# A cross-attention kernel: per-batch choice of block products, and where a bank is written back and a sum is formed

## The chip, the cores and the metric

The kernel runs on one core of a Trainium2 chip. The time is the device time of one execution in microseconds, median of three runs; lower is better. The core has TensorE for matrix products (PE in the profile; PEld is its weight load), VectorE (DVE), ScalarE (ACT), GpSimd (POOL) and SyncE (SP, here only a queue that issues DMAs). Each works off its own instructions in program order and waits for the others by semaphores.

## The reference

Eight batches of cross attention with a residual. Everything is float32. `x1` and `x2` are 512 x 1024 for each batch.

```python
def _L0_xattn_ref(x1, x2, Wq, bq, Wk, bk, Wv, bv):
    q = jnp.einsum('bcn,dc->bnd', x1, Wq) + bq
    k = jnp.einsum('bcn,dc->bdn', x2, Wk) + bk[:, None]
    v = jnp.einsum('bcn,dc->bdn', x2, Wv) + bv[:, None]
    attn = jax.nn.softmax(jnp.einsum('bnd,bdm->bnm', q, k), axis=2)
    attn_out = jnp.einsum('bcm,bnm->bcn', v, attn)
    return attn_out + x1
```

B = 8, C = 512, N = 1024, D = 64.

## The kernel before

The scores stand transposed (m on the partitions, n along the row), in two halves of n (`h` 0 and 1), each with four steps `i` of 2 x 128 rows. The kernel does not form v. It first multiplies x2 with the unnormalized exponentials (stage "y", inner dimension 1024), scales by the reciprocal of the column sums, and then multiplies Wv with that (stage "o", inner dimension 512). Both are 512 x 1024 results and both are done by a Strassen-Winograd scheme of seven products of quarters instead of eight (`MULT`, L382): product 1 is 11 by 11, product 2 is 12 by 21, 6 is S2 by T2, 7 is S3 by T3, 5 is S1 by T1, 3 is S4 by 22, 4 is 22 by T4. The S are sums of x2's quarters (`a` in the code), the T are sums of the quarters of the exponentials (`t`). S1 = 21 + 22, S2 = 11 - S1, S4 = 12 + S2, S3 = 11 - 21; T1 = 12 - 11, T2 = T1 - 22 with the signs of the code, T3 = 22 - 12, T4 = 21 + T2.

A product of the stage "y" can be done in two ways. **Whole**: `multiply` (L392), two rows j of 128, four inner steps each, 128x512 matmuls, onto the bank pair it belongs to; for products 1, 6, 5 ScalarE copies the bank's partial result into a tile `u6` or `u5` (L418). **In blocks**: the same seven-product scheme once more inside the product, with 128x256 matmuls: seven `inner_product`s (L470). It needs four sums of the left quarter (`inner_left`, L439, four VectorE instructions of 128x256) and the sums of the right one (`inner_right`, L451, one of 128x1024 and two of 128x512). There are two kinds of block products. `multiply_seeded` (L491) opens the banks: ScalarE copies partial results into them (L511), and `complete` adds a last part on VectorE (L517). `multiply_onto` (L521) adds onto banks that hold something, and collects the rest in a tile `d` (ScalarE copies, L483) with a `complete` on VectorE (L551). `multiply_joined` (L560) is that, plus two `join`s (L566) on VectorE that add the bank to `d`: afterwards `d` holds the running sum, and the bank does not. `reseed` (L570) has ScalarE write `d` back into the two `a` banks, so that the next product can go on from there.

`period` (L811) does one batch. `n`, `nn`, `nnn` are the next three. Work of the next batch stands inside: its scores (`scores_and`), maxima (`folds`, `fold_halves`, `highest`), exponentials. Batch numbers in the text count from the first (`s.b` = 0) to the eighth or last (`s.b` = 7). The line `six` (L814) says in which batches product 6 is done in blocks: the third to the sixth, and the last. Product 5 is done in blocks in all but the first. In the seventh there is no `nn`, in the last there is no `n`.

From the second batch on the order is: product 1 and 2 in blocks (`multiply_seeded`), with the folds for the sum of the second half's exponentials on VectorE (`adds`) and `total` (an all-reduce over partitions on GpSimd, L288, with a small DMA behind it); then 6, the scores of the next batch's first half, 5, 7, 3, the second half's scores, 4, and the stage "o". `hooks` are functions that are called between the inner products, which puts their instructions there in ScalarE's and GpSimd's order.

T3 is formed in place of the quarter 12: ScalarE negates half of it (`sum_t3`, L352), and a DMA from GpSimd's queue adds the quarter 22 (L356). The folds for the sum read the quarter 12 too. T4: ScalarE copies the quarter 21 (`copy_t4`, L346) and a DMA adds T2 (L350). S4: SyncE loads the quarter 12 (`begin_s4`, L167), a DMA on GpSimd's queue adds S2 (`end_s4`, L171). These DMAs move 512 KB each. All DMAs that add are on GpSimd's queue; so are those of the denominators: `invert` writes a row to DRAM (L298), `spread` reads it back to all partitions (L303). In the last batch T3 is formed by VectorE instead (`sum_e(s, "T3")`, two instructions at L331).

The banks: PSUM holds two double buffers `sc` (scores, and the two working buffers of a block product) and the pairs `a` and `c`. The second half's scores use the pair `a` for step 2 (L966); it has to be empty then, which `evict_t3` (L580, L583) does after product 3. `copy_u1` (L358) keeps product 1's banks in a tile, `evict_y` forms the quarters of the result, `scale_y` multiplies by the reciprocals.

`weave` (L274) emits lists of steps by turns. The order on each engine is the order in the program; no planner changes it.

Of the kernel before, what the change touches and what calls it, by code (L numbers as in the profile page):

```python
# [12 lines left out]
ALU = mybir.AluOpType  # L13
# [3 lines left out]
def kernel(  # L17
# [151 lines left out]
    def end_s4(s):  # L169

        nc.gpsimd.dma_start(s.a["S4"], s.a["S2"], accum_op=ALU.add)  # L171
# [98 lines left out]
    def folds(s, h, kind, op):  # L270

        return [lambda i=i: fold(s, h, i, kind, op) for i in range(1, MH)]

    def weave(*rows):  # L274

        for steps in zip_longest(*rows):
            for step in steps:
                if step:
                    step()
# [78 lines left out]
    def copy_u1(s, j):  # L358
        if j == 0:
            s.tmp[1] = sb.tile([P, 2, H], F32, tag="y21", name=f"uy1_{s.b}")  # L360
        nc.scalar.copy(s.tmp[1][:, j, :], s.bank["a", j])
# [77 lines left out]
    def inner_left(s, i, x, tag):  # L439

        v = {f"{p + 1}{q + 1}": x[:, ts(q, MH // 2), ts(p, P)] for p in range(2) for q in range(2)}
        sums = sb.tile([P, 4, MH // 2, P], F32, tag=tag, name=f"aI{i}_{s.b}")
        v |= {step[0]: sums[:, z] for z, step in enumerate(LEFT)}
        s.inner[i] = v

        def make(k, x, y, op):
            return lambda: nc.vector.tensor_tensor(v[k], v[x], v[y], op)

        return [make(*step) for step in LEFT]
# [110 lines left out]
    def multiply_joined(s, i, v_tag, hooks={}):  # L560

        s.tmp[i], complete = multiply_onto(s, i, f"u{i}", v_tag, hooks)

        def join(j):
            d = s.tmp[i][:, j, :]
            nc.vector.tensor_tensor(d, s.bank["a", j], d, ALU.add)  # L566

        return [complete, lambda: join(0), lambda: join(1)]

    def reseed(s):  # L570

        for j in range(2):
            nc.scalar.copy(s.bank["a", j], s.tmp[6][:, j, :])

    def copy_7(s, j):
        if j == 0:
# [234 lines left out]
    def period(s, n, nn, nnn):  # L811

        late = s.b >= 1
        six = late and (n is None or s.b >= 2 and nn is not None)  # L814

        def first(i):
            multiply(s, "y", i, s.a, s.t, MH)
# [19 lines left out]
        def scores_0():  # L837
            then = scores_and(n, 0, 1, "c", next_queries if nn else nothing)
            if six:
                reseed(s)  # L840
            return then

        def add_exponential(i):
# [44 lines left out]
            scale_y(s, "T3", "11", "22")  # L888
        else:
            complete_1 = multiply_seeded(s, 1, "y11")  # L890
            adds = folds(s, 1, "sum", ALU.add)
            if six:
                weave(
                    adds,
                    [nothing, complete_1] + inner_right(s, 6, s.t["T2"], "yT1", "yT2"),
                    [nothing, nothing] + inner_left(s, 6, s.a["S2"], "i2"),
                )
            else:
                weave(adds, [nothing, complete_1] + inner_left(s, 7, s.a["S3"], "yT4"))
            total(s, 1)  # L900
            hooks = {5: lambda: copy_u1(s, 0), 4: lambda: copy_u1(s, 1)}
            if n:
                hooks |= {6: lambda: sum_t3(s, 0), 3: lambda: sum_t3(s, 2)}
            complete_2 = multiply_seeded(s, 2, "y22", hooks)
            complete_2()
            evict_y(s, "11")
            invert(s, 0)
            begin_s4(s)
            end_s4(s)
            sum_t4(s)  # L910
            evict_q = None
            if six:
                hooks = {6: lambda: copy_t4(s, 0), 5: lambda: copy_t4(s, 2)}
                complete_6, *join_6 = multiply_joined(s, 6, "v", hooks)
                lefts_5 = [] if n else inner_left(s, 5, s.a["S1"], "a11")
                weave(
                    inner_right(s, 5, s.t["T1"], "y21", "u1"), lefts_5, inner_left(s, 7, s.a["S3"], "yT4")
                )
                complete_6()
                weave(join_6)  # L920
                if n:
                    evict_q = scores_0()
                    weave(inner_left(s, 5, s.a["S1"], "i2"))
                    weave(folds(n, 0, "max", ALU.max))
                else:
                    reseed(s)
                    sum_e(s, "T3")
            else:
                copy_t4(s, 0)
                copy_t4(s, 2)  # L930
                first(6)
                weave(inner_right(s, 5, s.t["T1"], "y21", "u1"), inner_left(s, 5, s.a["S1"], "i2"))
                evict_q = scores_0()
                weave(folds(n, 0, "max", ALU.max))
            rights_7 = inner_right(s, 7, s.t["T3"], "yT1", "yT2")
            weave(rights_7, [nothing, nothing] + inner_left(s, 3, s.a["S4"], "aI3"))
            complete_5, *join_5 = multiply_joined(s, 5, "r", {6: evict_q} if nn else {})
            complete_5()
            if n:
                fold_halves(n, 0, ALU.max)  # L940
                highest(n, 0)
            spread(s, 0)
            shares(s, 1)
            weave(join_5, inner_right(s, 3, s.t["22"], "eT1"))
            if n:
                lower(n, 0, 0)
            complete_7 = multiply_seeded(s, 7, "y12")
# [167 lines left out]
```

## Time and profile before

| what | value |
|---|---|
| median of 3 runs | 685.12 us (684.97 to 685.27) |
| profiled execution, its time | 684.92 us |
| its span, first to last instruction | 683.1 us |
| granted TensorE clock, mean | 0.997 |
| ScalarE busy | 345.8 us, 51% |
| GpSimd busy | 217.7 us, 32% |
| GpSimd's DMA queue (q0) | 58.27 MB, 47.3% of 16 engines' span |
| SyncE's DMA queue (q1) | 79.31 MB, 32.0% |
| DMA L356 (T3), 12 of 512 KB, issue to landing | 6.0 us median |
| DMA L171 (S4), 7 of 512 KB | 8.6 us median |
| DMA L350 (T4), 14 of 512 KB | 12.1 us median |

How to read it: a busy share is that of the whole span; the page's timeline gives for each instruction its start, its duration, and in brackets the idle time of its engine just before it with what ended that. Durations overlap their successors a little, so the steps from start to start are what counts: four 128x256 matmul instructions show 1.03 us and follow each other every 0.863.

### The profile page before, as it was taken

How to read it: one execution, taken by the hardware profiler on the slowest of the kernel's cores; microseconds unless marked ns; L12 is line 12 of the kernel's file. 1: busy time of each engine (PE TensorE's matmuls, PEld its weight loads, DVE VectorE, ACT ScalarE, POOL GpSimd, SP SyncE). 2: the span in 40 equal slices, each digit the busy share in tenths (PEclk: the TensorE clock that was granted, in tenths of full speed). 3: DMA queues.
4: the chain of work that ended last, by engine and by line, in shares of the span. 5: the costliest groups of instructions: out<-in, count | busy, mean ns of one | idle time of the engine just before them, and what ended most of it. 6: DMA issues, size and time to landing. Idle time of an engine off the chain costs nothing.

```text
span 683.1 us, 7499 instructions
## 1 busy us (share of the span) xinstructions
PE 669.0 (98%) x2504; PEld 415.0 (61%) x2504; DVE 625.4 (92%) x826; ACT 345.8 (51%) x595; POOL 217.7 (32%) x189
## 2 busy tenths in 40 slices
PE   9999999999999999999999999999999999995997
PEld 5333554756558665668647685486755676474863
DVE  1999998989999999999999999999999889999884
ACT  2734266546455564473754656545645548443320
POOL 0124215341435314451144512434143621443100
PEclk9999999999999999999999999999999999999999
DMA  9666658997996969969699796998789784498503
GB/s 302 267 204 228 153 214 146 253 192 229 249 246 186 228 181 292 227 183 262 172 277 237 162 284 171 257 249 155 233 197 192 222 174 73 93 207 264 120 14 110
DMA packets 52790, 138.45 MB, mean 203 GB/s; under 512 B 5776, under 2 KB 8080, under 8 KB 52752
## 3 DMA queue, kind: packets, MB, share of 16 engines
q0 software_dynamic: 23472, 58.27, 47.3%
q1 hardware_dynamic: 28992, 79.31, 32.0%
q10 hardware_dynamic: 288, 0.39, 0.2%
q8 instruction: 20, 0.33, 0.2%
q14 instruction: 18, 0.15, 0.1%
HBM read 90.97 MB, written 16.81 MB: 158 GB/s over the span
## 4 chain that ended last, share of the span: by engine, by line
PE 93%; DVE 4%; DMA 1%; ACT 1%; issue 1%; SPq 0%; DVEq 0%; ACTq 0%
PE ps_oa L407 12%; PE ps_ya L474 10%; PE ps_oc L407 8%; PE ps_yc L474 8%; PE ps_s L240 6%; PE ps_ya L407 5%; PE ps_o L407 4%; PE ps_o L427 4%; PE ps_q L193 4%; PE ps_k L193 3%; PE ps_i4chain L474 3%; PE ps_i3chain L474 3%; PE ps_i5chain L474 3%; PE ps_i7chain L474 3%; PE ps_i1chain L474 3%; PE ps_i2chain L474 2%
## 5 line engine op out<-in xcount | busy, mean ns | idle before, releaser
L288 POOL PARTITION_ALL_REDUCE den<-half x16 | 51.6, 3225 | 91.2 <-DVE half L268 91.2
L283 POOL PARTITION_ALL_REDUCE top<-max x16 | 31.7, 1980 | 131.3 <-DVE few L296 58.2
L318 DVE TENSOR_TENSOR e<-e,top 128x1024 f32<-128x1024 f32 x60 | 69.8, 1213 | 0.0
L322 ACT ACTIVATE e<-e 128x1024 f32<-128x1024 f32 x60 | 61.8, 1057 | 6.2 <-DVE e L318 5.5
L407 PE MATMUL ps_oa<-yT,w_S 128*128 128x512 f32 x128 | 57.5, 592 | 0.0
L407 PE MATMUL ps_oc<-yT,w 128*128 128x512 f32 x128 | 57.4, 592 | 0.0
L667 POOL DMA_DIRECT2D sum<-e x21 | 28.9, 1377 | 84.3 <-ACT sum L672 36.1
L249 ACT COPY e<-ps_s 128x1024 f32<-128x1024 f32 x46 | 45.6, 1031 | 12.2 <-PE ps_s L240 7.2
L240 PE MATMUL ps_s<-q,k 64*128 64x512 f32 x188 | 47.8, 608 | 0.9 <-ACT q L693 0.8
L407 PEld LDWEIGHTS ps_oa<-yT,w_S 128*128 128x128 f32 x128 | 24.3, 190 | 30.6 <-issue 30.6
L407 PEld LDWEIGHTS ps_oc<-yT,w 128*128 128x128 f32 x128 | 24.3, 190 | 30.6 <-issue 29.9
L260 DVE TENSOR_TENSOR max<-max,e 128x1024 f32<-128x1024 f32 x30 | 36.7, 1222 | 2.2 <-DVE max L260 0.5
L418 ACT COPY uo<-ps_oa 128x512 f32<-128x512 f32 x32 | 18.7, 585 | 35.1 <-PE ps_oa L407 34.0
L240 PEld LDWEIGHTS ps_s<-q,k 64*128 64x128 f32 x188 | 17.0, 186 | 23.0 <-issue 16.3
L511 ACT COPY ps_ya<-ps_i1chain 128x256 f32<-128x256 f32 x28 | 10.0, 357 | 40.8 <-PE ps_i1chain L474 37.3
L588 DVE TENSOR_TENSOR y<-y,den 128x1024 f32<-128x1024 f32 x24 | 30.4, 1293 | 0.3
L407 PE MATMUL ps_oa<-y,w_S 128*128 128x512 f32 (+1 forms) x68 | 28.8, 567 | 0.0
L407 PE MATMUL ps_o<-y,w 128*128 128x512 f32 x64 | 28.8, 592 | 0.0
L427 PE MATMUL ps_o<-y,w 128*128 128x512 f32 x64 | 28.8, 592 | 0.0
L407 PE MATMUL ps_ya<-eT,aS 128*128 128x512 f32 x64 | 28.3, 595 | 0.0
L193 PE MATMUL ps_k<-x_in_x_dram,wqk_sb 128*64 128x512 f32 x112 | 26.0, 600 | 0.4 <-DMA x_in_x_dram<-in_x_dram 0.4
L331 DVE TENSOR_TENSOR eT<-eT,e 128x1024 f32<-128x1024 f32 x16 | 26.1, 1637 | 0.0
(217 smaller groups left out, 1655.1 us busy)
## 6 DMA issues: line engine op xcount, KB each, us to landing
x_in_x_dram<-in_x_dram SPq DMA_DIRECT2D x60, 512.0 KB, 8.4
a<-in_x2T_dram SPq DMA_DIRECT2D x32, 512.0 KB, 9.9
sum<-e POOLq DMA_DIRECT2D x21, 512.0 KB, 9.1
aS<-in_x2T_dram SPq DMA_DIRECT2D x14, 512.0 KB, 6.3
aS<-in_x2T_dram POOLq DMA_DIRECT2D x14, 512.0 KB, 7.6
uo<-in_x_dram POOLq DMA_DIRECT2D x14, 512.0 KB, 10.4
r<-in_x_dram POOLq DMA_DIRECT2D x14, 512.0 KB, 11.2
out_dram<-r SPq DMA_DIRECT2D x14, 512.0 KB, 4.6
```

What stands on the lines that cost most here:

```text
L193: nc.tensor.matmul(ps[r, :], w_sb[:, c, :], s.x[:, c, ts(h, H)], start=(c == 0), stop=(c == CT - 1),)
L240: nc.tensor.matmul(ps[g], s.k[r, ts(i, P)], s.q[r, ts(h, H)], start=True, stop=True)
L249: nc.scalar.copy(e[:, :, i, :], whole)
L260: nc.vector.tensor_tensor(f, e[:, :, 0, :] if i == 1 else f, e[:, :, i, :], op)
L283: nc.gpsimd.partition_all_reduce(s.top[h], s.half[h], P, ReduceOp.max)
L288: nc.gpsimd.partition_all_reduce(s.den[h], s.half[h], P, ReduceOp.add)
L318: nc.vector.tensor_tensor(e, e, top, ALU.subtract)
L322: nc.scalar.activation(e, e, AF.Exp)
L407: nc.tensor.matmul(ps[:, n], left[ka][:, k, ts(j, P)], right[kb][:, k, n], start=opens and k == 0, stop=i in (2, 3, 4) and k == n_k - 1, s ...
L427: nc.tensor.matmul(ps, w["11"][:, k, ts(j, P)], s.y["11"][:, k, :], start=k == 0, stop=False, skip_group_check=True)
L474: nc.tensor.matmul(ps, s.inner[i][ka][:, k, :], s.inner[i, "t"][kb][:, k, :], start=opens and k == 0, stop=z in (2, 3, 4) and k == MH // 2 ...
L588: nc.vector.tensor_tensor(s.y[k], s.y[k], rden, ALU.mult)
```

## The change

- `six` now also holds for the second batch: product 6 in blocks there. A new `five`, with the same condition, says where product 5 is done in blocks: all batches from the second but the seventh, which does it whole.
- `multiply_joined` returns its steps in the order first join, `complete`, second join (before: `complete`, first, second).
- `reseed` writes back one bank at a time. In the last batch its two calls are hooks inside product 5, behind its first and third inner product (1 and 6); before, both stood ahead of product 5. In the other batches they stay behind the scores.
- Where product 6 is in blocks, its sums and product 1's `complete` come behind the first of the three folds of the exponentials' sum; the other two folds follow them. `total` is issued behind product 2's inner products.
- T3's first half is a hook of product 2 in all batches from the second, the last included, so GpSimd issues its DMA ahead of the all-reduce. Its second half moves from a hook of product 2 to one of product 6 (with T4's second half), or, in the seventh batch, in front of product 6. The last batch no longer forms T3 on VectorE.
- `end_s4` moves behind product 6's inner products and their hooks (in the seventh batch behind T4's copies).
- The left sums of product 7 are no longer woven with the right sums of product 5, but follow them; in the last batch they follow the joins of product 6.
- The joins of product 5 are issued ahead of `spread` and `shares`, no longer woven with the right sums of product 3.

```diff
-        return [complete, lambda: join(0), lambda: join(1)]
-
-    def reseed(s):
-
-        for j in range(2):
-            nc.scalar.copy(s.bank["a", j], s.tmp[6][:, j, :])
+        return [lambda: join(0), complete, lambda: join(1)]
+
+    def reseed(s, j):
+
+        nc.scalar.copy(s.bank["a", j], s.tmp[6][:, j, :])
...
-        six = late and (n is None or s.b >= 2 and nn is not None)
+        six = five = late and (n is None or nn is not None)
...
             if six:
-                reseed(s)
+                for j in range(2):
+                    reseed(s, j)
             return then
...
             complete_1 = multiply_seeded(s, 1, "y11")
-            adds = folds(s, 1, "sum", ALU.add)
+            add_1, *adds = folds(s, 1, "sum", ALU.add)
             if six:
-                weave(
-                    adds,
-                    [nothing, complete_1] + inner_right(s, 6, s.t["T2"], "yT1", "yT2"),
-                    [nothing, nothing] + inner_left(s, 6, s.a["S2"], "i2"),
-                )
+                add_1()
+                complete_1()
+                weave(inner_right(s, 6, s.t["T2"], "yT1", "yT2"), inner_left(s, 6, s.a["S2"], "i2"))
+                weave(adds)
             else:
-                weave(adds, [nothing, complete_1] + inner_left(s, 7, s.a["S3"], "yT4"))
+                weave([add_1] + adds, [nothing, complete_1] + inner_left(s, 7, s.a["S3"], "yT4"))
+            hooks = {
+                6: lambda: sum_t3(s, 0), 5: lambda: copy_u1(s, 0), 4: lambda: copy_u1(s, 1)
+            }
+            complete_2 = multiply_seeded(s, 2, "y22", hooks)
             total(s, 1)
-            hooks = {5: lambda: copy_u1(s, 0), 4: lambda: copy_u1(s, 1)}
-            if n:
-                hooks |= {6: lambda: sum_t3(s, 0), 3: lambda: sum_t3(s, 2)}
-            complete_2 = multiply_seeded(s, 2, "y22", hooks)
             complete_2()
             evict_y(s, "11")
             invert(s, 0)
             begin_s4(s)
-            end_s4(s)
             sum_t4(s)
+
+            def more():
+                sum_t3(s, 2)
+                copy_t4(s, 2)
+
             evict_q = None
             if six:
-                hooks = {6: lambda: copy_t4(s, 0), 5: lambda: copy_t4(s, 2)}
-                complete_6, *join_6 = multiply_joined(s, 6, "v", hooks)
+                join_6 = multiply_joined(s, 6, "v", {6: lambda: copy_t4(s, 0), 5: more})
+                end_s4(s)
                 lefts_5 = [] if n else inner_left(s, 5, s.a["S1"], "a11")
-                weave(
-                    inner_right(s, 5, s.t["T1"], "y21", "u1"), lefts_5, inner_left(s, 7, s.a["S3"], "yT4")
-                )
-                complete_6()
-                weave(join_6)
+                weave(inner_right(s, 5, s.t["T1"], "y21", "u1"), lefts_5)
                 if n:
+                    weave(inner_left(s, 7, s.a["S3"], "yT4"))
+                    weave(join_6)
                     evict_q = scores_0()
                     weave(inner_left(s, 5, s.a["S1"], "i2"))
                     weave(folds(n, 0, "max", ALU.max))
                 else:
-                    reseed(s)
-                    sum_e(s, "T3")
+                    weave(join_6)
+                    weave(inner_left(s, 7, s.a["S3"], "yT4"))
             else:
+                more()
                 copy_t4(s, 0)
-                copy_t4(s, 2)
+                end_s4(s)
                 first(6)
-                weave(inner_right(s, 5, s.t["T1"], "y21", "u1"), inner_left(s, 5, s.a["S1"], "i2"))
                 evict_q = scores_0()
                 weave(folds(n, 0, "max", ALU.max))
-            rights_7 = inner_right(s, 7, s.t["T3"], "yT1", "yT2")
-            weave(rights_7, [nothing, nothing] + inner_left(s, 3, s.a["S4"], "aI3"))
-            complete_5, *join_5 = multiply_joined(s, 5, "r", {6: evict_q} if nn else {})
-            complete_5()
+            weave(
+                inner_right(s, 7, s.t["T3"], "yT1", "yT2"),
+                [nothing, nothing] + inner_left(s, 3, s.a["S4"], "aI3"),
+            )
+            if five:
+                hooks = {6: evict_q} if nn else {}
+                if n is None:
+                    hooks = {1: lambda: reseed(s, 0), 6: lambda: reseed(s, 1)}
+                first_5, complete_5, second_5 = multiply_joined(s, 5, "r", hooks)
+                complete_5()
+                join_5 = [first_5, second_5]
+            else:
+                first(5)
+                join_5 = []
             if n:
                 fold_halves(n, 0, ALU.max)
                 highest(n, 0)
+            weave(join_5)
             spread(s, 0)
             shares(s, 1)
-            weave(join_5, inner_right(s, 3, s.t["22"], "eT1"))
+            weave(inner_right(s, 3, s.t["22"], "eT1"))
```

## The prediction

> **What bounds the kernel now.** I read the page's head and chain of waits first, then the waits by engine, then the timelines of TensorE, VectorE and GpSimd batch by batch (the batches' first products begin at 120.1, 202.1, 283.3, 364.4, 445.6, 526.8 and 603.3 us for the second to the eighth).
>
> ```profile
> span 683.1 us, 7499 instructions
> ...
> PE 669.0 (98%) x2504; PEld 415.0 (61%) x2504; DVE 625.4 (92%) x826; ACT 345.8 (51%) x595; POOL 217.7 (32%) x189
> ...
> PE 93%; DVE 4%; DMA 1%; ACT 1%; issue 1%; SPq 0%; DVEq 0%; ACTq 0%
> ```
>
> TensorE sets the time, with VectorE close behind at 92%. The waits of TensorE say where that fails: nearly all of its idle time is in the last batch.
>
> ```profile
> PE ps_i5chain L474 <- ACT d L483: 4.8, 1, 4.8
> PE ps_i6third L474 <- DVE aI L447: 1.5, 1, 1.5
> ...
> PE ps_i6chain L474 <- DVE aI L447: 0.8, 1, 0.8
> PE ps_i5chain L474 <- ACT e L249: 0.5, 1, 0.5
> ```
>
> The first three belong to the eighth batch, the last to the seventh. From the TensorE timeline: four matmuls of 128x512 go every 1.72 us (16 in 6.87), a block product of 28 instructions of 128x256 takes 28 x 0.2157 = 6.04 us, a whole one 6.87.
>
> In the third to sixth batch TensorE never waits, but VectorE has hardly any room. Shown is the third:
>
> ```profile
> 231.77 0.75 DVE L447 TENSOR_TENSOR aI<-aS 128x256 f32<-128x256 f32 x2
> ...
> 245.53 0.70 DVE L517 TENSOR_TENSOR ps_ya<-ps_ya,v 128x512 f32<-128x512 f32 x1 [0.42 <-ACT ps_ya L511]
> 246.14 1.28 DVE L583 TENSOR_TENSOR yT<-uy,ps_ya 128x512 f32<-128x512 f32 x2
> ...
> 247.69 1.02 PE L240 MATMUL ps_sa<-q,k 64*128 64x512 f32 x4
> ```
>
> At 231.77 VectorE reads S4 (the left sums of product 3). At 246.14 to 247.42 it empties the two `a` banks, which the scores at 247.69 (second half some 0.43 later, 248.1) write again. So a delay of VectorE behind 231.77 is free up to 0.42 (its idle time) plus 0.7 (248.1 less 247.42), 1.1 us together; what is beyond stops TensorE. The same rows stand in the fourth to sixth batch.
>
> **Part 1: GpSimd's queue, all batches from the second on.** Before, the order behind the reciprocal is T3 (both halves, L356), the row of the denominators, S4's sum (L171), T4's two halves (L350):
>
> ```profile
> 220.21 1.79 POOL L356 DMA_DIRECT2D e<-e  x2
> 221.33 1.24 POOL L298 DMA_DIRECT2D row<-few  x1
> 221.89 1.55 POOL L171 DMA_DIRECT2D aS<-aS  x1
> 222.43 2.75 POOL L350 DMA_DIRECT2D eT<-eT  x2
> ```
>
> The views of these lines give the landings:
>
> ```profile
> L350 POOL DMA_DIRECT2D eT<-eT x2: 1882/2048/2214, 222.4 to 223.0; - x2
> ...
> DMA to landing us min/median/max: 11.8/13.9/16.1
> ```
>
> L356 takes 4.8 and 7.1 us, L171 8.6. So the five transfers of 512 KB land at 225.0, 227.9, 230.5, 234.2 and 239.1: one after another, 2.6 to 4.9 us apart. After the change T3's first half goes out ahead of the all-reduce (ScalarE negates it at 211.2), and behind the row come T4(0), T3(2), T4(2) and only then S4, since `end_s4` is issued behind product 6 with its hooks. GpSimd is still held by the all-reduce until 219.33; few at 219.63, row 220.21, T4(0) 220.77, T3(2) 221.33, T4(2) 221.9, S4 222.46. S4 goes from third to fourth. Two rows give the fourth's landing: 11.8 us from its issue (234.3), or, in the seventh batch, where no loads of x run beside it, L350's first 10.5 us from an issue at 544.9, 12.7 behind the start of the group (220.77 + 12.7 = 233.5). Counted from the start of the group the third batch's row is 14.0 (234.8). I take 234.4, with 233.5 and 234.8 as ends. T3(2), second in line, lands at 228.4, ahead of its reader at 229.2.
>
> The Trainium skill speaks against this: "DMA: Bandwidth & Descriptors", section "Anatomy of one DMA — SWDGE (gpsimd) path", fits a transfer of this path as 2.0 us plus bytes by 436 GB/s, that is 1.2 us for each 512 KB; four in a row would be an estimated 6.8 us, S4 would land at 227.6 and nothing would wait (the sum would be that of the third rival below). The rows above, 4.8 us for a first and 12.7 to 14.0 for a fourth, decide against it.
>
> VectorE is strictly in order: behind the S4 sums wait product 5's `complete`, the fold for the maximum, the right sums of product 3, the lowering of the scores, the evictions. They all come 234.4 - 231.77 = 2.6 us later, plus 0.1 for the reordered joins (results that are read at once, 0.12 per pair as in the steps of 1.25 against 1.13 in the folds). Less the free 1.1: **1.6 us for each of four batches, 6.4** (ends 0.7 and 2.0 each, 2.8 and 8.0).
>
> **Part 2: the second batch, product 6 in blocks.** TensorE gains 6.87 - 6.04 = 0.83. VectorE gets the seven sums (third batch: 211.51 to 215.32, 3.81 us) and `complete` with two joins (222.00 to 223.81, 1.81): 5.62, and some 0.5 of read-at-once gaps from the new order. Its idle time on this stretch:
>
> ```profile
> 142.42 1.22 DVE L260 TENSOR_TENSOR max<-e 128x1024 f32<-128x1024 f32 x1 [1.79 <-ACT e L247]
> ...
> 146.90 1.22 DVE L463 TENSOR_TENSOR eI7yT<-e 128x1024 f32<-128x1024 f32 x1 [0.59 <-DMA e<-e]
> ...
> 151.67 0.69 DVE L551 TENSOR_TENSOR d<-d,v 128x512 f32<-128x512 f32 x1 [0.51 <-ACT d L483]
> ...
> 164.36 0.70 DVE L517 TENSOR_TENSOR ps_ya<-ps_ya,v 128x512 f32<-128x512 f32 x1 [0.78 <-ACT ps_ya L511]
> ```
>
> Together 3.67. VectorE enters this batch 2.75 us later than the third (its first sum is 8.04 us behind the batch's start against 5.29), so it can't take the rest: the bank is emptied 5.62 + 0.5 - 3.67 = 2.45 later; 0.7 of that is free, 1.75 moves the scores. The 0.83 saved only lengthens TensorE's wait. Then part 1: S4 is issued at about 143.3 and lands 11.7 later (that batch's row), 155.0, against a reader at 149.49 + 5.62 + 0.45 - 2.38 = 153.2: 1.8 more. **+3.55** (ends: 2.85 and 4.15 with S4 12.7 and 14.0 behind its group's start at 141.6; 1.75 if it is in time).
>
> **Part 3: the seventh batch, product 5 whole.** TensorE +0.83, but product 5 no longer needs the score buffers, so the 0.50 wait goes and its slower first groups: 550.02 to 556.23 becomes 549.5 to 556.4. **+0.2** (ends 0 and 0.83). VectorE loses seven sums (in front of a 4.53 us idle) and 1.8 us of `complete` and joins; some 0.5 of that is lost to S4 (fourth at 555.9, read at 555.47), and some 0.5 reaches the last batch, as evictions and one transfer (608.08, waiting 0.63 for a sum) stand between.
>
> **Part 4: the last batch.** Before:
>
> ```profile
> 629.75 2.34 DVE L331 TENSOR_TENSOR e<-e 128x1024 f32<-128x1024 f32 x2
> ...
> 630.86 2.07 PE L474 MATMUL ps_i5chain<-eI5u,aI 128*128 128x256 f32 x4 [4.77 <-ACT d L483]
> ```
>
> Product 6's sums now stand ahead of two folds (2.4 us): its waits of 1.7 and 1.0 (starts against 0.863 steps) go, and it ends near 621.6 instead of 625.1. Product 5 follows at once, but its own sums start behind folds, total and eviction: at 622.1, slowed by the all-reduce, so TensorE waits about 1.8 for the first, 1.0 for S2, 0.7 for the first write-back (join at 626.9, copy 0.55), and ends near 631.1 instead of 637.0: 5.9 earlier. Product 7 then wants T3. Its second half goes out at 625.65 behind T4(0) at 625.1, and a second in line lands 7.7 behind the first's issue (7.1 + 0.56): 632.8, against VectorE's 632.13 before. So product 7 stalls 2.3, and the lead is 3.5. From there VectorE is the chain: right sums of 7, left of 3, joins, right sums of 3, the blocks of 4, T3's eviction, scaling, y21. It ends 1.7 earlier than before; product 2 of the output stage, which had 0.86 of slack, starts 2.5 earlier if T3 lands at 632.8, 1.3 earlier if at 634 (the loads of x run beside). **-2.2** (ends -3.5, T3 in time, and 0).
>
> The clock: the 4.77 us wait was followed by two groups of 1.87 and 1.64 instead of 0.863 (1.78 lost, inside the -5.9), the waits of 1.54 and 0.77 by none. No row lies between; I take no slow groups, up to 1.8 if there are some. The skill's "TensorE: Matmul & The Clock Gate", section "HAM oscillation — how this bites in real kernels", puts the bound at idle gaps over some 3.4 us; by it the new waits cost nothing more, which is the same sum.
>
> **Sum**: 6.4 + 3.55 + 0.2 - 2.2 = +7.95 on the profiled execution's 684.92 (span 683.1 and 1.8 around it): 692.9. The median of the runs lies 0.20 above that execution: **693.1**. With the ends of the S4 landing alone (2.8 and 2.85, or 8.0 and 4.15, for parts 1 and 2): 688.8 to 695.3.
>
> **Rivals.**
> - The last batch gives nothing: T3 lands past 634 beside the loads of x, and the pieces of waiting slow the clock (1.8). For it: DMA's busy share is 0.82 in 620 to 635 already. 693.1 + 2.2 = 695.3, up to 697.
> - Faster, by one mechanism: the shorter group on GpSimd's queue drains sooner than its rows say. It decides if S4 lands before 232.2, that is within 9.7 us of its issue, and T3 before 629.8. Then part 1 is 0, part 2 is 1.75, the last batch -3.5: 1.75 + 0.2 - 3.5 = -1.55, 683.6; if VectorE's gaps in the second batch are smaller too, 682. For it: one 512 KB transfer leaves the group. Against: a third one took 10.3 us from the group's start in every batch.
> - S4 in time, T3 not: 1.75 + 0.2 - 2.2 = -0.25, 684.9; no change that shows.
>
> **Chances.** Forecast 0.60, last batch without gain 0.15, faster 0.17, no change 0.08. A measurement of this kernel tells about 0.2% (1.4 us) from no change. Faster 0.17, same 0.08, slower 0.75. The range 684.0 to 697.5 leaves out most of the faster case and what lies over the first rival; the likeliest case's own range is 688.8 to 695.3.
>
> **What would show it.** In the third to sixth batch a VectorE wait of about 2 us at L447 for the transfer aS<-aS, and TensorE waiting 1 to 2 us at L240 ps_sa for L583; batches 82.8 us apart instead of 81.2. In the second the same, larger. In the last no wait of 4.8, several of 0.7 to 2.3, and VectorE waiting for e<-e. Wrong, if L447 doesn't wait for S4 and the batches stay 81.2 apart.

## The result, and the profile after

| | before | after |
|---|---|---|
| median | 685.19 us (684.97 to 685.57, 4 runs) | 706.09 us (705.73 to 706.28, 4 runs) |
| ratio | | 1.0304 [1.0286, 1.0322] |
| profiled execution, its span | 684.92, 683.1 | 706.28, 704.4 |
| granted TensorE clock, mean | 0.997 | 0.988 |

The change makes the kernel 3.0% slower; 693.1 was forecast, with 697.5 as the upper end. The direction was right, the size was not: 13.0 us more than forecast.

The page's head and the chain of waits of the changed kernel:

```profile
span 704.4 us, 7500 instructions
...
PE 678.8 (96%) x2504; PEld 418.2 (59%) x2504; DVE 624.3 (89%) x824; ACT 351.0 (50%) x599; POOL 220.5 (31%) x191
...
PE 65%; DMA 15%; DVE 9%; POOL 4%; issue 4%; ACT 1%; SPq 1%; DVEq 0%; POOLq 0%
```

TensorE had 93% of the chain before and DMA 1%; now TensorE has 65% and DMA 15%. VectorE's busy time is nearly unchanged (625.4 to 624.3 us), so this isn't more work but more waiting. The waits (engine, what it was about to write, its line, what released it; total, times, longest):

```profile
DVE aI L447 <- DMA aS<-aS: 18.1, 6, 4.1
...
PE ps_i3third L474 <- DVE eI3eT L463: 7.0, 4, 4.1
DVE eI7yT L463 <- DMA e<-e: 6.0, 1, 6.0
PE ps_sa L240 <- DVE yT L582: 5.0, 4, 1.3
```

VectorE waits 18.1 us for S4's sum, in six batches. Before it was 0.3.

Taken from the first block of product 1 in each batch (the head is the first batch; the last one reaches to the end of the span):

```
             1st     2nd     3rd     4th     5th     6th     7th     last    span
before     120.11   81.99   81.17   81.16   81.17   81.17   76.51   79.82   683.1
after      120.87   87.91   84.04   83.65   84.38   83.66   76.42   83.47   704.4
difference  +0.76   +5.92   +2.87   +2.49   +3.21   +2.49   -0.09   +3.65   +21.3
forecast      0     +3.55   +1.6    +1.6    +1.6    +1.6    +0.2    -2.2    +7.95
```

The next table says when VectorE begins the left sums of product 3 (L447, its first reading of S4), counted from the batch's start, and how long the batch goes on from there:

```
             2nd     3rd     4th     5th     6th     last
before      29.38   29.67   29.67   29.68   29.68   31.87
after       37.31   33.45   33.06   33.79   33.07   37.58
goes on,
  before    52.61   51.50   51.49   51.49   51.49   47.95
  after     50.60   50.59   50.59   50.59   50.59   45.89
```

After the change the rest is 50.6 us in every batch from the second to the sixth, however late S4 is: what VectorE loses there is passed on whole.

**Third batch**, timeline of after, answering to the lines at 221.89, 231.77, 246.14 and 247.69 before:

```profile
229.25 1.88 POOL L171 DMA_DIRECT2D aS<-aS  x1
...
242.23 0.76 DVE L447 TENSOR_TENSOR aI<-aS 128x256 f32<-128x256 f32 x2 [3.06 <-DMA aS<-aS]
...
255.82 1.27 DVE L582 TENSOR_TENSOR yT<-uy,ps_ya 128x512 f32<-128x512 f32 x2
...
256.55 1.29 PE L240 MATMUL ps_sa<-q,k 64*128 64x512 f32 x3 [1.25 <-DVE yT L582]
```

S4 is issued at 229.25 and lands 13.0 us later, at 242.2. VectorE idles 3.06 us for it and shows no wait after that until the two `a` banks are empty at 257.09. TensorE loses time in three places. In product 3, which needs VectorE's right sums, it is 0.76 us. In front of the scores that write the `a` banks it is 1.42, of which the line shows 1.25 as waiting. The rest of the scores takes 2.51 us (from 256.55 to the next line's start at 259.06) where it took 1.81 (247.69 to 249.50), 0.70 more, since the second bank comes later still. Together these are the batch's 2.87 but for rounding.

**Second batch**, same view:

```profile
158.18 0.76 DVE L447 TENSOR_TENSOR aI<-aS 128x256 f32<-128x256 f32 x2 [4.10 <-DMA aS<-aS]
...
163.61 2.05 PE L474 MATMUL ps_i3third<-eI3eT,aI 128*128 128x256 f32 x4 [4.07 <-DVE eI3eT L463]
165.44 1.91 PE L474 MATMUL ps_i3chain<-eI3eT,aI 128*128 128x256 f32 x4
167.15 1.71 PE L474 MATMUL ps_ya<-e,aS 128*128 128x256 f32 x4
168.69 1.03 PE L474 MATMUL ps_i3chain<-eI3eT,aI 128*128 128x256 f32 x4
...
171.76 1.27 DVE L582 TENSOR_TENSOR yT<-uy,ps_ya 128x512 f32<-128x512 f32 x2
...
173.20 1.02 PE L240 MATMUL ps_sa<-q,k 64*128 64x512 f32 x4
```

Here the delay reaches TensorE at product 3 itself: 4.07 us idle, and then three groups whose steps are 1.83, 1.71 and 1.54 us instead of 0.863, which is 2.5 us more. The granted clock from 163.61 to 168.69 is 0.52. The sum 4.07 + 2.5 - 0.83 (product 6 in blocks) is 5.7 of the batch's 5.92, but it is not what sets the batch's length. VectorE shows no wait from 158.18 until the banks are empty at 173.03, 14.85 us, and the scores that write them begin at 173.20. With S4 second on the queue (an experiment below) no group of this batch is slow, and VectorE takes the same 14.84 us; from S4's sums on that batch goes on for 50.57 us, this one for 50.60. So what is paid for is VectorE's wait of 4.10, and TensorE is slow in time that it would have spent waiting.

**Last batch**, same view:

```profile
639.77 0.59 SPq L167 DMA_DIRECT2D aS<-in_x2T_dram  x1
...
641.89 1.10 PE L474 MATMUL ps_i5third<-eI5y,aI 128*128 128x256 f32 x4 [1.80 <-DVE aI L447]
...
643.33 1.22 POOL L356 DMA_DIRECT2D e<-e  x1
643.77 2.04 PE L474 MATMUL ps_i5chain<-eI5u,aI 128*128 128x256 f32 x4 [0.78 <-DVE aI L447]
...
650.13 0.83 POOL L171 DMA_DIRECT2D aS<-aS  x1 [4.71 <-DMA aS<-in_x2T_dram]
...
653.59 1.22 DVE L463 TENSOR_TENSOR eI7yT<-e 128x1024 f32<-128x1024 f32 x1 [5.99 <-DMA e<-e]
...
658.51 0.76 DVE L447 TENSOR_TENSOR aI<-aS 128x256 f32<-128x256 f32 x2 [2.25 <-DMA aS<-aS]
```

Product 6 runs without a wait, and the 4.77 us wait is gone. But four groups of product 5 are slow behind the waits of 1.80 and 0.78 (steps 1.83, 1.71, 1.71, 1.25: 3.1 us more); T3's second half, issued at 643.33, takes 10.2 us and holds VectorE for 5.99; S4's own load goes out at 639.77 behind four loads of x, and GpSimd waits 4.71 for it. That wait stood in the kernel before too (4.70). But there the load went out 17.84 us behind the batch's start and took 8.5, and the sum 4.9; here it goes out 18.84 behind the start and takes 9.8, and the sum, now behind T3's and T4's, 8.4. Product 5 ends 30.2 us after the batch's start (33.7 before), but the stage "o" begins 55.4 after it (51.8 before).

The chain that ended last, in order of time, says which of these waits the batch pays for:

```profile
639.77 9.80 DMA aS<-in_x2T_dram
...
650.13 8.36 DMA aS<-aS
...
658.51 0.77 DVE aI L447 x2
...
662.08 1.12 DVE eI3eT L463
...
663.34 1.94 PE ps_i3third L474 x4
```

It goes through S4's load and S4's sum. The slow groups of product 5 aren't on it: TensorE waits 2.79 us for product 7's sums behind them. T3 isn't either, but stands close behind: without the wait of 2.25 VectorE would have come to S4's sums at 656.26, still 3.5 later behind the batch's start than before. By the second table VectorE begins S4's sums 5.71 us later than before and the batch goes on 2.06 less from there, which gives the 3.65.

### The profile page after: what moved, and what is told of

It is laid out like the page before. It is cut to its first block, busy times and chain, and to the rows that moved or that the text cites. A ratio compares the mean times of both kernels' runs of the same rounds, so it can differ in the third digit from the quotient of the medians.

```text
span 704.4 us, 7500 instructions
## 1 busy us (share of the span) xinstructions
PE 678.8 (96%) x2504; PEld 418.2 (59%) x2504; DVE 624.3 (89%) x824; ACT 351.0 (50%) x599; POOL 220.5 (31%) x191
## 4 chain that ended last, share of the span: by engine, by line
PE 65%; DMA 15%; DVE 9%; POOL 4%; issue 4%; ACT 1%; SPq 1%; DVEq 0%; POOLq 0%
PE ps_oa L407 12%; DMA aS<-aS 10%; PE ps_oc L407 8%; PE ps_ya L407 5%; PE ps_ya L474 5%; PE ps_yc L474 5%; PE ps_o L407 4%; PE ps_o L427 4%; PE ps_k L193 3%; PE ps_i4chain L474 3%; PE ps_i1chain L474 3%; PE ps_s L240 3%; PE ps_i2chain L474 2%; DVE e L318 2%; POOL den L288 2%
## 5 line engine op out<-in xcount | busy, mean ns | idle before, releaser
L240 PE MATMUL ps_s<-q,k 64*128 64x512 f32 x188 | 49.6, 608 | 0.8 <-ACT q L692 0.8
L447 DVE TENSOR_TENSOR aI<-aS 128x256 f32<-128x256 f32 x40 | 15.7, 417 | 18.2 <-DMA aS<-aS 18.1
L240 PEld LDWEIGHTS ps_s<-q,k 64*128 64x128 f32 x188 | 18.1, 186 | 21.9 <-issue 15.9
```

The costliest lines, as they stand in the source:

```text
L240: nc.tensor.matmul(ps[g], s.k[r, ts(i, P)], s.q[r, ts(h, H)], start=True, stop=True)
```

## The experiments

The theory: in each batch, the place of S4's sum on GpSimd's queue sets the loss; the last batch loses by T3 and S4, which both land late. The first rival: it is the new order of VectorE's and ScalarE's work. All lengths of batches below are from the profiled execution of each kernel; medians and ratios are from all its runs, against the kernel before on the same chip.

**S4 first on the queue.** The sum stands directly behind its load again, for all batches:

```diff
             begin_s4(s)
+            end_s4(s)
             sum_t4(s)
...
                 join_6 = multiply_joined(s, 6, "v", {6: lambda: copy_t4(s, 0), 5: more})
-                end_s4(s)
...
                 copy_t4(s, 0)
-                end_s4(s)
                 first(6)
```

> The changed kernel with S4's sum issued directly behind its load, so first of the four transfers on GpSimd's queue (then T4(0), T3(2), T4(2)). Theory (S4's place on that queue costs the third to sixth batch 2.5 to 3.2 us each, by VectorE's wait at L447 for aS<-aS): that wait goes; T3's second half, now third, lands some 10.5 us behind the group's start against a reader at about 9, so a wait of 0 to 2 for e<-e may stand in its place; these batches fall from 83.7-84.4 to 81.2-82.2, the second by 2 to 4, the whole to 692 to 698. Rival (the new order of VectorE's and ScalarE's work costs it, S4's wait only fills time that is lost anyway): these batches stay at 83 or more, the whole at 704 or more.

**T3's second half first, S4 second**, and T4's halves, which nobody needs before product 4, behind both:

```diff
-            def more():
-                sum_t3(s, 2)
-                copy_t4(s, 2)
+            def some():
+                sum_t3(s, 2)
+                end_s4(s)
+
+            def more():
+                copy_t4(s, 0)
+                copy_t4(s, 2)
...
-                join_6 = multiply_joined(s, 6, "v", {6: lambda: copy_t4(s, 0), 5: more})
-                end_s4(s)
+                join_6 = multiply_joined(s, 6, "v", {6: some, 5: more})
...
-                more()
-                copy_t4(s, 0)
-                end_s4(s)
+                some()
+                more()
                 first(6)
```

> The changed kernel with the order T3(2), S4, T4(0), T4(2) on GpSimd's queue. Theory (S4's place): neither S4 nor T3 is waited for; the third to sixth batch return to 81.2 us as before, the second to 82 to 85, the whole comes to 689 to 695, with the last batch still 2 to 3.7 longer than before. Rival (order of VectorE's and ScalarE's work): 83 or more per batch, the whole at 704 or more.

```
             1st     2nd     3rd     4th     5th     6th     7th     last    span
S4 first   120.17   88.33   84.16   82.56   85.47   82.27   76.42   88.72   708.1
S4 second  119.72   83.69   81.17   81.17   81.17   81.17   76.42   80.49   685.0
```

S4 first: 709.79 us, 1.0358 [1.0342, 1.0373]. The expected 692 to 698 was wrong. The wait for S4 did go, but a wait of the same size took its place. Third batch of this kernel:

```profile
229.08 1.52 POOL L356 DMA_DIRECT2D e<-e  x1
...
239.48 1.23 DVE L463 TENSOR_TENSOR eI7yT<-e 128x1024 f32<-128x1024 f32 x1 [3.19 <-DMA e<-e]
```

T3's second half is now third and lands 10.4 us from its issue, 11.5 from the group's start at 227.96. I had put its reader at 9 behind that start and the third's landing at 10.5; what was the wait for S4 is now 3.19 us for T3, and S4's sums, which stand behind T3's on VectorE, begin as late as in the changed kernel (33.58 us behind the batch's start, there 33.45). In the last batch it is worse: S4's sum stands at the head of the queue until 648.48 (S4's load goes out at 638.03 and takes 9.9), T3 behind it until 649.60, and TensorE waits 12.0 us for product 7's sums.

S4 second: 686.57 us, 1.0021 [1.0012, 1.0031]. All four middle batches are back at 81.17, the value before, with the changed order of VectorE's and ScalarE's work left as it is. So that order costs the middle batches nothing, and the order of the four transfers all of the 2.5 to 3.2 us. This settles the first rival.

**The fourth place by itself**, in the kernel before: its queue T3(0), T3(2), S4, T4(0), T4(2) with S4 and T4(0) exchanged.

```diff
             begin_s4(s)
-            end_s4(s)
...
-                hooks = {6: lambda: copy_t4(s, 0), 5: lambda: copy_t4(s, 2)}
+                def more():
+                    end_s4(s)
+                    copy_t4(s, 2)
+
+                hooks = {6: lambda: copy_t4(s, 0), 5: more}
...
                 copy_t4(s, 0)
+                end_s4(s)
                 copy_t4(s, 2)
```

> The kernel before with one edit: S4's sum goes out behind T4's first half instead of ahead of it, so fourth of the five transfers T3(0), T3(2), T4(0), S4, T4(2) instead of third. It prices the fourth place by itself. The prediction's term: landing 12.7 to 14.0 us from the group's start, VectorE 2.6 late, third to sixth batch 1.6 longer each (82.8), the whole at 691 to 693. Rival, what the changed kernel's batches show (landing 14.6 from the group's start): 2.5 to 3.2 longer each, the whole at 695 to 699. Third: the fourth of these is in time (landing below 11.6): under 0.3 each, the whole at 685.

695.11 us, 1.0151 [1.0136, 1.0166]. Third, fourth and sixth batch 82.99, 82.99 and 82.98 (+1.8), fifth 84.19 (+3.0), second 83.84 (+1.85). In the third batch:

```profile
224.36 1.88 POOL L171 DMA_DIRECT2D aS<-aS  x1
...
236.12 0.76 DVE L447 TENSOR_TENSOR aI<-aS 128x256 f32<-128x256 f32 x2 [2.34 <-DMA aS<-aS]
```

Landing 11.8 us from the issue, 14.0 from the group's start at 222.13: the end of the range that the prediction read from this batch. The cost of 1.8 a batch is close to the predicted 1.6, in part by luck: S4's sums begin 2.44 later than before (2.6 predicted), and only 0.6 of that is free (1.1 predicted). In the changed kernel S4 is issued at the same distance from the batch's start (20.47 us, here 20.35), but its group starts 0.7 later (18.81 against 18.12; the row of the denominators goes ahead), and it lands 1.3 later (33.4 against 32.1 from the batch's start). From S4's sums on, this kernel's batch goes on for 50.88 us and the changed one's for 50.59, by its other order of VectorE's work. So 1.3 less 0.3 is the difference between 1.8 and 2.9 in the third batch. In the fifth batch of this kernel S4 lands 33.3 us behind the start, 1.2 later than in the third, and that batch is 1.2 longer; why S4 is later there wasn't tried.

**Second and seventh batch alone**, in the kernel before:

```diff
-        six = late and (n is None or s.b >= 2 and nn is not None)
+        six = late and (n is None or nn is not None)
...
                 first(6)
-                weave(inner_right(s, 5, s.t["T1"], "y21", "u1"), inner_left(s, 5, s.a["S1"], "i2"))
...
-            complete_5, *join_5 = multiply_joined(s, 5, "r", {6: evict_q} if nn else {})
-            complete_5()
+            if six:
+                complete_5, *join_5 = multiply_joined(s, 5, "r", {6: evict_q} if nn else {})
+                complete_5()
+            else:
+                first(5)
+                join_5 = []
```

> The kernel before with only the second batch's product 6 in blocks and the seventh's product 5 whole; the order on GpSimd's queue is that of before. Theory of the prediction (VectorE is the bound of the second batch; S4's lateness comes on top of it): second batch 1.75 us longer, seventh 0.2, the whole at 687.1. Rival (TensorE's 0.83 saved shows): second batch 0.8 shorter, seventh up to 0.8 longer, the whole at 685.2. Other rival (a wait of over 3 us in front of product 3 slows the clock without S4 having a part in it): second batch 4 to 6 longer, the whole at 689 to 691.

686.53 us, 1.0021 [1.0012, 1.0031]. Second batch 83.42 (+1.43, expected +1.75), seventh 76.43 (-0.08, expected +0.2). VectorE is the bound of the second batch, and TensorE's 0.83 doesn't show. With S4 second on the queue the second batch was 83.69; the changed kernel has 87.91. So of its +5.92, 1.4 to 1.7 is VectorE's work and 4.2 is S4's place: VectorE's wait of 4.10 and little more. The slow groups stand in neither of the two kernels where S4 is in time, but as said above they cost this batch nothing.

**The last batch alone**: the first seven batches by the function `period` of before, the eighth by that of after.

```diff
+    def period(s, *later):
+        (period_after if s.b in (7,) else period_before)(s, *later)
```

> The kernel before in the first seven batches, the changed kernel's code in the last batch alone. Theory (the last batch loses 3.65 us by itself: slow clock in product 5, T3 10.2 us on the way, S4 behind the loads of x): the whole 3 to 4 us above before, 688.2 to 689.2. Rival (the last batch alone is the gain of 2.2 that was predicted, and what the batches in front of it hand over spoils it): 683.

689.29 us, 1.0061 [1.0044, 1.0078]; last batch 84.20 (+4.4). It loses by itself, nothing that the batches in front hand over is needed for it.

**What the last batch waits for.** With S4 second on the queue it takes 80.49. From there: T3's second half by VectorE again (one instruction of 1.2 us), or the loads of x behind S4's load, or both; the one with both also has the second batch's product 6 whole, as before.

```diff
-                sum_t3(s, 2)
+                if n:
+                    sum_t3(s, 2)
                 end_s4(s)
...
+            if n is None:
+                sums_e(s, "T3")[1]()
             weave(
                 inner_right(s, 7, s.t["T3"], "yT1", "yT2"),
```

> As the kernel with T3(2) and S4 first on GpSimd's queue (last batch 80.5 us), but the last batch's second half of T3 is subtracted by VectorE (1.2 us) instead of ScalarE and a DMA. Theory (the last batch waits for two transfers that the four loads of x hold up, T3's first and S4's right behind): the wait for e<-e goes, but S4 still lands near 35 us after the batch's start, so VectorE's wait at L447 for aS<-aS grows to 3 to 4 and the last batch stays at 79 to 80.5. Rival (T3's DMA alone is what the last batch loses): it falls by 2.8 to 4, to 76.5 to 77.7.

```diff
-        if n is None:
-            load_x(s, x1)
...
             begin_s4(s)
+            if n is None:
+                load_x(s, x1)
             sum_t4(s)
```

> As the kernel with T3(2) and S4 first on GpSimd's queue, but the last batch's loads of x are issued behind S4's load instead of ahead of all. Theory (the loads of x hold up T3 and S4): S4's load lands 5 us or more sooner, T3(2) comes in 5 to 7.5 us from its issue instead of 9.5; PE's wait for eI7yT falls from 2.8 to below 1, the last batch from 80.5 to 76.5-78.5. Rival (the transfers of the group are slow by themselves, x doesn't matter): 80 or more.

> Both of these together, and the second batch as in the kernel before (product 6 whole). Second batch 82.0, third to sixth 81.2, seventh 76.4. Theory: the last batch keeps only the waits of 1.8 and 0.8 in product 5 with the slow groups behind them, and comes to 76 to 77.5; the whole to 681 to 682.5, faster than the kernel before. Rival (another transfer or VectorE takes over): last batch at 79 or more, the whole at 684 or more.

| kernel | median | ratio to before | profiled execution | its last batch | S4's sums begin, behind its start | TensorE's longest wait there |
|---|---|---|---|---|---|---|
| S4 second | 686.57 | 1.0021 [1.0012, 1.0031] | 686.76 | 80.49 | 35.29 | 2.8, product 7's sums (T3) |
| T3(2) by VectorE | 686.13 | 1.0018 [1.0009, 1.0028] | 685.94 | 79.68 | 33.55 | 3.0, product 3's right sums, behind S4's left ones |
| x later | 685.65 | 1.0013 [1.0001, 1.0025] | 684.06 | 77.95 | 32.77 | 1.8, product 7's sums (T3) |
| both, second batch as before | 680.78 | 0.9942 [0.9925, 0.9958] | 680.66 | 75.98 | 30.79 | 1.4, product 5's sums |

The last batch follows S4's sums here too: from them on it goes on for 45.2 us in three of the four kernels, and for 46.1 in the second one, where slow groups stand in product 3. Each change alone gives little: T3's wait goes and S4's takes its place, or T3 still takes 8.3 us from its issue. The profiled execution of the third kernel is the quickest of ten that reach to 687.84, so by the medians x is worth 0.9 and not 2.5. Both together give 5.8 us by the medians, of which the second batch's 1.7 is known; 4.1 stay for the last batch. That version is 0.58% faster than the kernel before and beats both. Its last batch is 3.84 shorter than before's, and the seventh one 0.08.

The Trainium skill's "DMA: Bandwidth & Descriptors", section "Queues, rings and completion order", says that the DMA engines serve the rows that have work by turns, so a load on one queue and a sum on another share them. The runs agree as far as they go: T3(2) of the last batch took 9.4 us with the loads of x just ahead (S4 second), 8.3 with them behind S4's load (x later); no run here took the loads away.

**Is the clock what slows product 5?** In the version with both, as in the changed kernel, two short waits are followed by slow groups:

```profile
623.50 1.10 PE L474 MATMUL ps_i5third<-eI5y,aI 128*128 128x256 f32 x4 [1.43 <-DVE aI L447]
625.37 2.05 PE L474 MATMUL ps_i5chain<-eI5u,aI 128*128 128x256 f32 x4 [0.77 <-DVE aI L447]
627.21 1.79 PE L474 MATMUL ps_ya<-eT,aS 128*128 128x256 f32 x4
```

The granted clock from 625.37 to 628.84 is 0.51. Two kernels put matmuls into those waits, in front of the real ones and with product 5's first operands, that write an unused half of a score buffer:

```diff
+        if s.b == B - 1 and i == 5 and z in (7, 6):
+            for k in range(8 if z == 7 else 4):
+                nc.tensor.matmul(
+                    s.fill,
+                    s.inner[i]["11"][:, k % 2, :],
+                    s.inner[i, "t"]["11"][:, k % 2, :],
+                    start=k == 0,
+                    stop=True,
+                    skip_group_check=True,
+                )
         for k in range(MH // 2):
```

> The same with matmuls that nobody reads (eight and four of 128x256, into a free half of a score buffer) ahead of the two groups of the last batch's product 5 that wait for VectorE. If the idle 1.8 and 0.8 us cause the slow groups that follow, those steps of 1.6 to 1.8 us return to 0.86 and the last batch is 1 to 2 us shorter than without. Rival (the clock falls for another reason, or the filling only delays the real groups): same time or up to 0.7 longer.

```diff
-        if s.b == B - 1 and i == 5 and z in (7, 6):
-            for k in range(8 if z == 7 else 4):
+        if s.b == B - 1 and i == 5 and z == 7:
+            for k in range(3):
```

> The kernel with T3(2) by VectorE and x later, with unread matmuls (six passes of 128x256, 1.3 us) in the first idle stretch of the last batch's product 5 only, so that they end before the sums they wait beside. If the idle time causes the slow groups behind it: the steps of 1.84 and 1.63 us become 0.86, last batch 1.0 to 1.75 shorter than 75.98, the whole 679 to 680. Rival (a remaining idle of 0.8 is enough for the slow groups): the same time as without, 680.8.

The first: 682.08 us, 0.9956 [0.9941, 0.9971], last batch 77.35. Each of these matmuls is two instructions, so the first filling takes 3.5 us where 1.4 were idle, and the second waits 1.36 itself: the real groups are delayed. But every one of them has its step of 0.863, and the granted clock is 1.0. The second:

```profile
622.09 1.46 PE L475 MATMUL ps_i5third<-eT,aS 128*128 128x256 f32 x6
623.82 1.13 PE L484 MATMUL ps_i5third<-eI5y,aI 128*128 128x256 f32 x4 [0.27 <-DVE aI L447]
625.78 1.10 PE L484 MATMUL ps_i5chain<-eI5u,aI 128*128 128x256 f32 x4 [0.84 <-DVE aI L447]
```

No slow group follows (start to start 1.59 and 0.97, of which 0.49 of waiting for a write-back; 1.84 and 1.63 without the filling), and the granted clock from 625.37 to 628.84 is 1.00. So it is the idle time that slows them, by the clock. Yet the time is the same: 680.85, 0.9943 [0.993, 0.9957], last batch 75.90, against an expected 679 to 680. The wait for a write-back (0.49) and small ones for product 7's and product 3's sums (0.19 and 0.26) show instead: VectorE is as late as before (S4's sums begin 30.77 us behind the batch's start, 30.79 without the filling), and TensorE's speed between isn't what ends last there.

**Folds later.** So VectorE's work in front of product 5 was moved: the last batch's folds and their all-reduce behind product 5's sums and joins.

```diff
-                weave(adds)
+                if n:
+                    weave(adds)
...
-            total(s, 1)
+            if n:
+                total(s, 1)
             complete_2()
...
                 else:
                     weave(join_6)
+                    weave(adds)
+                    total(s, 1)
```

> The same kernel without the unread matmuls; the last batch's folds of the denominator (2.5 us on VectorE) and their all-reduce go behind product 5's sums and joins. Product 5's waits of 1.4 and 0.8 go, and with them the slow groups (1.75): 3.9 less there. T3's second half and product 7's right sums then come 1 to 2.5 later than TensorE wants them. Theory: last batch 1.5 to 2.5 shorter than 75.98, the whole at 678 to 679.5. Rival (the wait moves to product 7 in full): 75 to 76.5, the whole at 680 to 681.

683.97 us, 0.9985 [0.9976, 0.9994]; last batch 78.50. Product 5 runs without its two waits for sums, but T3's second half and product 7's sums come so late that TensorE waits 5.96 us there, and two slow groups follow (1.5 us more). Both cases expected less; the move loses 3.2 us to the version without it.

## Why the prediction was wrong

That the kernel gets slower was right, and so was the path in the second to sixth batch: VectorE waits for S4, and TensorE for VectorE. What failed there is the size of one term, the time at which S4 lands. In the last batch the path failed: the sum has no wait for S4 in it, and the batch pays for that one and for T3.

- **Part 1, S4 fourth on GpSimd's queue, 1.6 a batch; measured 2.5 to 3.2 (11.1 instead of 6.4).** The mechanism is the one that was named: moving S4 alone, in the kernel before, costs 1.8 a batch, and putting it second in the changed kernel brings back 81.17 to the digit. What was mis-sized is the landing "I take 234.4": 32.3 us behind the batch's start, measured 33.4 in the third batch and 33.1 to 33.8 in the next three. The group of four starts 0.7 later than its predecessor, since the denominators' row is now ahead of it; the prediction had that start right (220.77), but chose between rows of landings that are counted from different points; even its upper end, 14.0 from the group's start, was short of the 14.6 measured. So S4's sums begin 3.8 us later than before, not 2.6. The free 1.1 was too much: the third batch is 2.87 longer, so 0.9 was free, and 0.6 where S4 alone was moved.
- The Trainium skill's "DMA: Bandwidth & Descriptors", section "Anatomy of one DMA — SWDGE (gpsimd) path", had been weighed against those rows. By its fit of 2.0 us plus bytes by 436 GB/s a fourth transfer of 512 KB would be an estimated 6.8 us behind the first's issue; 14.0 and 14.6 were measured. From the group's start to S4's landing (227.59 to 242.23) the DMA engines are busy for 0.96 of the time and move 195 GB/s, all queues together. The measurement decides, and the third rival, S4 in time, falls with the estimate.
- **Part 2, second batch, +3.55; measured +5.92.** VectorE's share, 1.75, was 1.4 to 1.7 when measured alone. S4's share was taken as 1.8 and is 4.2. The reader was ready when the sum said (33.2 us behind the batch's start, 33.1 forecast), but S4 was to land 11.7 us from its issue, 34.9 behind the start, and took 14.0, 37.3 behind the start. These 2.4 are all that the term lacks. That TensorE stops at product 3 already, for 4.07 us, and is slow behind it, wasn't foreseen and costs no more.
- **Part 3, +0.2; measured -0.09**, and -0.08 alone.
- **Part 4, last batch, -2.2; measured +3.65.** The step that failed is "From there VectorE is the chain: right sums of 7, left of 3": the left sums of product 3 read S4, and the sum has them follow at once. With T3 at 632.8 they would have begun at 635.5, 32.2 us behind the batch's start; they began at 37.6. Of these 5.4 us, 3.1 are T3's second half. It lands 10.2 us from its own issue, where the forecast had 7.7 from the issue of the transfer ahead of it: it was priced from the third batch, where the loads of x begin only as it lands (227.65), and here four of them go out from 636.06 on, ahead of it. The other 2.25 are S4, which the sum puts at nothing, though its load stands behind x's on SyncE's queue and its sum now behind T3's and T4's. "I take no slow groups" was wrong too: they take 3.1 us more in product 5 and 1.7 in product 3. But the first are followed by a wait, and behind the second the batch goes on for 45.9 us from S4's sums, against 45.2 in kernels without them, so they cost some 0.7. The rival "the last batch gives nothing" named T3 and the clock, but not S4, and capped the loss at 1.8 on top of no gain.
- The remaining 0.76 is in the first batch, whose code isn't changed. Over the thirteen profiles it lies between 119.6 and 120.9; the changed kernel's is the highest of them. It isn't put down to the change.
- The faster rival fell: S4 was never within 9.7 us of its issue in the second to sixth batch (12.4 to 14.0).

## What to carry to other kernels

Transfers that are issued one behind another on one queue land one behind another, so order them by when their readers want them, and price each by its distance from the start of its group: here the same four transfers cost the four middle batches 11 us or nothing. An instruction on such a queue that waits for a load (S4's sum) holds all that stands behind it, so ask for each load what is ahead of it on its own queue too. When a reader gets its data late, ask whether that engine has idle time behind it. Where it has none, it passes the delay on whole (here 50.6 us from S4's sums to the batch's end, in every middle batch), and what another engine loses meanwhile, slow groups too, isn't added on top as long as that engine would only have waited.

## What the runs showed of the hardware

**Slow groups behind idle TensorE.** In the second and last batches of the thirteen profiles, all nine waits of 3.0 us or more (3.01 to 12.0) were followed by two to three groups of slow steps, 1.5 to 2.5 us more in sum. But of the nine pairs of a wait of 1.25 to 1.91 and one of 0.73 to 0.78 behind it, six were too, and three (1.54, 1.65, 1.69) were not; single waits of 2.10 and 2.78 were, others of 1.83 and 2.79 were not. The granted clock over such groups is about 0.5 (0.52 from 163.61 to 168.69 in the changed kernel). The "TensorE: Matmul & The Clock Gate" page of the Trainium skill, section "HAM oscillation — how this bites in real kernels", has waits in front of the matmuls let the clock fall; the prediction used it with a bound of 3.4 us for one gap. The runs differ from that bound: single waits of 2.10 to 3.08 us, and two short ones within some 4 us, can do the same. What decides there stays open.

**A slow clock that costs nothing.** With the idle stretch filled the slow groups vanish and the time stays (680.85 and 680.78): behind them stands VectorE, and TensorE would only have waited there. The second batch of the changed kernel shows the same: with 2.5 us of slow groups it goes on for 50.60 us from S4's sums, and without any, with S4 second on the queue, for 50.57.
